# Filling the joints of a four-layer kernel: first steps, last steps, and where square roots and turned tiles go

## The chip, the cores and the metric

The kernel runs on one core of a Trainium2 chip. A core has TensorE (PE; its weight loads are listed apart as PEld), VectorE (DVE), ScalarE (ACT), GpSimd (POOL) and SyncE (SP), which here only issues transfers. Each engine works off its own queue in order. The metric is the time of one execution on the device, in microseconds. The kernel before takes 2728.55 us, the median of three runs (2726.72 to 2733.25).

## The reference, cut to what matters

All is float32. The tokens are x, 16 batches of 100 rows of 512 numbers (1600 rows, 13 tiles of 128 rows). Every batch has its own context of 722 rows of 384 numbers. Four layers are added to x one after the other:

```python
x = x + tanh(g_xattn[0]) * attention0(layernorm(x), ctx)    # 16 heads of 32, biases
x = x + tanh(g_ffn[0])   * experts(layernorm(x))            # 8 experts, the top 2 of each token
x = x + tanh(g_xattn[1]) * attention1(layernorm(x), ctx)    # 8 heads of 64
x = x + tanh(g_ffn[1])   * quantized_ffn(layernorm(x))      # its own residual and normalization inside
```

Attention is queries times keys, softmax, times values, and a projection. The experts' layer picks two experts of each token, computes silu(x w0) * (x w1) wo, and weighs the two results. The last layer is h + 0.5 * (silu(norm(h) w1 + b1) w2 + b2), with w1 and w2 of int32 and a scale for each group of 128 rows, so the input of this layer is normalized twice.

## The kernel before, in words

**Attention (class Attention).** The work is cut into 64 steps: 16 batches of 4 groups m of 128 columns. For a step, `scores` multiplies keys and queries into PSUM (one tile "s"), ACT copies them to SBUF (line 386), and two DVE reductions and a maximum (389, 384) give `mx`. `peaks` turns mx on PE (399) and DVE reduces it to the peak (405). `softmax` spreads the peak on PE (413); DVE subtracts it in two parts (421), ACT takes the exponential of each part (427), and POOL (first attention) or DVE (second) adds up the sums (430). `attend` multiplies with the values (442, 453), and DVE divides (461, 462) into the buffer tT. `project` multiplies a finished tile of 128 tokens with Wo (468) and adds it to x (475).

PE's order is the order in which the program is written. `run` emits, for step i, the peaks of step i, the scores of step i+1, the attend of step i-1, the softmax of step i, and in between a share of other work that does not hang on the chain. That other work is: `extra`, a list of units with a step written beside each (query inputs, queries, projections and whatever the caller adds as `more`), and `todo`, the keys and values of the later batches. Every unit has a `cost` in columns; what is left is divided by the steps that are left, and units of `todo` are added until the share is filled or until their `last` step has come. `cut` puts the first units (2000 columns) ahead of the softmax. Up to `late`, the step before the last but one, an attend follows one step behind; the last three attends are held back. A batch's values come in 6 chunks of 6 matmuls each; its keys in 8 units of 6 matmuls.

**PSUM.** All short products of an attention ("mm") share four tiles in turn: a new one waits until the product four places earlier has been read.

**The other engines' order** is made by a planner, which takes an instruction as soon as its inputs and its buffer are expected to be there, even far ahead of its place in the program. So the last layer's first moments run at 1716 us, long before that layer. A DMA or a POOL instruction that needs SBUF held by an earlier tile waits until that tile's last reader is done: the last layer's pools lie at the same addresses as the second attention's.

**Around the attentions.** `query_input` normalizes a tile of tokens, `transposed` turns it on PE (139) and DVE copies it from PSUM (140). `norm_scales` is a square root on ACT (117), a reciprocal and a product on DVE (118, 119). ACT holds the table of one set of functions: a square root between exponentials is preceded and followed by a table load.

The first attention starts with `first_keys`, values of chunks 0 to 3 of batch 0, `output_bias`, the four query inputs, and the first queries; chunks 4 and 5 follow in step 0. After each group of projected tiles the experts' input is normalized, turned (`Experts.turn`) and multiplied with the gate's weights (`logits`); `top_two` picks the experts, for tiles 0 to 9 in step 60, and for 10 to 12 after the attention, where `places` and `row_map` then sort the tokens. The second attention's run begins with `summed`, which gathers each token's two expert rows by an indirect DMA, adds them to x (970), and takes moments and norm_scales of that one tile; tiles 4 to 12 come in steps 1 to 9.

**The last layer (quantized_ffn)** takes four groups FG of tiles. `normal` takes moments and scales, normalizes a tile on POOL (124), mixes it into x on DVE (1050), takes moments and scales of the result, normalizes on POOL again and adds a bias on POOL (1059). `turn` transposes four 128-column pieces (1071) and DVE writes hT (1076). `weights` loads integers and scales and dequantizes them on DVE (1033); the integers have one buffer. `feed` runs 16 hidden pieces (1095) and their second products (1113).

Of the kernel before, what the change touches and what calls it, by code (L numbers as in the profile page):

```python
# [68 lines left out]
class Layers:  # L69
# [63 lines left out]
    def transposed(self, psum, out, src):  # L133

        nc = self.nc
        n, r = out.shape[1], out.shape[2]
        ps = psum.tile([P, n, r], F32, tag="mm", name="ps_tr")
        for k in range(n):
            nc.tensor.transpose(ps[:, k, :], src[:, k * P : (k + 1) * P], self.ident[:r, :r])  # L139
        nc.vector.tensor_copy(out, ps)  # L140


class Attention:
# [170 lines left out]
    def query_input(self, i, on_act=False, bias=True):  # L314
# [14 lines left out]
        net.transposed(self.ps_m, self.tT[:, :, i * P : i * P + n], xn[:n])  # L329
# [152 lines left out]
    def cost(self, unit):  # L482

        f = unit[0].__name__
        cols = {"values": 6 * C, "keys": 6 * SH, "queries": 8 * GT, "project": 8 * C}
# [10 lines left out]
    def run(self, done=(), after_project=None, more=()):  # L496
# [8 lines left out]
        for g in range(1, B // GB):  # L505
            at = 4 * KC * (g - 1)
            for n, i in enumerate(range(last_tile(g - 1) + 1, last_tile(g) + 1)):
                extra[at + 3 + n].append((self.query_input, i))
# [22 lines left out]
        def last(unit):  # L531

            f, b, n = unit[:3]
            return 4 * b + n - 2 if f == self.keys else 4 * b + (b == B - 1)
# [4 lines left out]
        late = len(steps) - 2  # L539
# [48 lines left out]
class Experts:  # L588
# [71 lines left out]
    def turn(self, psum, p2, i):  # L660
        n = rows_of(i)
        self.xnT[i] = p2.tile([P, KC, P], F32, tag="xnT", name=f"xnT_moe_{i}")
        self.net.transposed(psum, self.xnT[i][:, :, :n], self.xn.pop(i)[:n])
# [318 lines left out]
def quantized_ffn(net, p, gate, out):  # L982
# [3 lines left out]
    with ExitStack() as ctx:  # L986
        pool = lambda n, k, **kw: open_pool(ctx, tc, f"ffn_{n}", k, **kw)

        ps, pq, px, ph, p1, p2 = (
            pool("s", 1), pool("q", 1), pool("x", 4), pool("h", 2), pool("1", 1), pool("2", 2),  # L990
        )
        ps_t, ps_y, ps_z = (pool(n, k, space=PSUM) for n, k in (("t", 2), ("y", 2), ("z", 4)))
        small = {}
        for n in ("gamma_cols", "beta_cols", "b1_cols"):
            small[n] = ps.tile(list(p[n].shape), F32, name=f"ffn_{n}")
            nc.sync.dma_start(small[n], p[n])
        b2 = ps.tile([P, C], F32, name="ffn_b2")
        nc.sync.dma_start(b2, p["b2"].partition_broadcast(P))
        hg = ps.tile([P, 1], F32, name="ffn_hg")
        nc.vector.tensor_scalar(hg, gate, 0.5, None, ALU.mult)  # L1000
        nc.vector.tensor_scalar(b2, b2, hg, None, ALU.mult)
# [35 lines left out]
        xn = {}  # L1037

        def normal(tiles):
# [7 lines left out]
            for i in tiles:  # L1047
                xn[i] = px.tile([P, C], F32, tag="xn", name=f"xn_ffn_{i}")
                net.normalized(nc.gpsimd, xn[i], i)
                nc.vector.scalar_tensor_tensor(  # L1050
                    x[:, i, :], xn[i], gate, x[:, i, :], ALU.mult, ALU.add
                )
            for i in tiles:
                net.moments(i, xn[i])
            net.norm_scales(a, z)
            for i in tiles:
                net.normalized(nc.gpsimd, xn[i], i, xn[i])
# [573 lines left out]
```

## Time and profile before

| what | value |
|---|---|
| median of three runs | 2728.55 us |
| profiled execution, its own time | 2728.79 us |
| its span, first to last instruction | 2727.1 us |
| PE busy | 2682.2 us (98%) |
| mean granted clock of PE | 0.992 |
| first attention | 0 to about 897 us |
| routing | about 897 to 945 us |
| experts | about 945 to 1573 us |
| second attention | about 1573 to 2359 us |
| last layer | about 2359 to 2727 us |

A timeline row reads: start, duration, engine, line, operation, written tile <- read tiles, shape, count, and in brackets the idle time ahead of it with what ended it. In a row of windows the numbers are the stretch, its length, the busy time of PE, PEld, DVE, ACT and POOL with the instructions of each, the granted clock of PE (1.00 is full speed), the share of the DMA engines and GB/s.

### The profile page before, as it was taken

Reading aid. Unit: us, or ns where it says so; the run is one execution under the profiler, and the core shown is the slowest. Engines: PE = TensorE matmul, PEld = TensorE weight load, DVE = VectorE, ACT = ScalarE, POOL = GpSimd, SP = SyncE. Lnnn points to the kernel's source line nnn. Section 1 sums busy time; section 2 is a strip of 40 time slices with the busy share of each in tenths; the row PEclk is TensorE's granted clock in tenths of the full one; section 3 lists DMA queues with packets and bytes.
Section 4 is the critical chain, followed back from the end, with each engine's and each line's share of the span. In section 5 each row is a group of like instructions: output and inputs, shape, how many; then the busy total and the mean of one; then the engine's idle time right before and its main releaser. Section 6 shows DMA issues by size and latency. Waiting matters only on the chain. (4 is left out here: it accounts for less than half of the span.)

```text
span 2727.1 us, 45782 instructions
## 1 busy us (share of the span) xinstructions
PE 2682.2 (98%) x19716; PEld 1739.5 (64%) x19716; DVE 1201.4 (44%) x2010; ACT 860.3 (32%) x1194; POOL 500.2 (18%) x497
## 2 busy tenths in 40 slices
PE   8999999999998999999999999999999999999999
PEld 5666666666565688888888865666666666445554
DVE  4666666666667310101010067656555556711100
ACT  3545554545455100000000045333333334311110
POOL 2544444444442000000000042000000000301000
PEclk9999999999999899999999999999999999999999
DMA  4001000010001499898999522001001010610000
GB/s 167 18 18 34 18 29 22 19 44 18 18 29 58 148 362 353 315 319 314 320 313 317 187 86 68 21 17 34 17 17 34 17 33 1 186 62 16 12 12 10
DMA packets 129189, 278.33 MB, mean 102 GB/s; under 512 B 5824, under 2 KB 5840, under 8 KB 128464
## 3 DMA queue, kind: packets, MB, share of 16 engines
q1 hardware_dynamic: 117888, 246.80, 26.2%
q0 software_dynamic: 5968, 19.17, 2.1%
q10 hardware_dynamic: 5120, 9.31, 0.9%
q8 instruction: 160, 2.62, 0.4%
q14 instruction: 53, 0.43, 0.0%
HBM read 260.31 MB, written 14.94 MB: 101 GB/s over the span
## 5 line engine op out<-in xcount | busy, mean ns | idle before, releaser
L241 PE MATMUL ps_v<-wv_a,ctx_a 128*128 128x512 f32 (+1 forms) x1152 | 520.8, 599 | 1.0 <-DVE pT L421 0.5
L216 PE MATMUL ps_k<-ctx_a,wk_a 128*128 128x361 f32 x1488 | 486.1, 474 | 3.0 <-DVE pT L421 2.3
L887 PE MATMUL ps_h<-xT,w 128*128 128x128 f32 x3712 | 421.8, 276 | 4.0 <-DVEq L1516 4.0
L887 PEld LDWEIGHTS ps_h<-xT,w 128*128 128x128 f32 x3712 | 419.3, 193 | 4.7 <-issue 4.7
L216 PEld LDWEIGHTS ps_k<-ctx_a,wk_a 128*128 128x128 f32 x1488 | 273.6, 190 | 165.7 <-issue 20.5
L241 PEld LDWEIGHTS ps_v<-wv_a,ctx_a 128*128 128x128 f32 (+1 forms) x1152 | 204.2, 184 | 240.9 <-issue 227.4
L427 ACT ACTIVATE pT<-pT 128x1200 f32<-128x1200 f32 (+1 forms) x256 | 243.2, 953 | 248.7 <-DVE pT L421 239.5
L421 DVE TENSOR_TENSOR pT<-raw_a,ps_top 128x400 f32<-128x400 f32 (+4 forms) x384 | 278.7, 770 | 11.5 <-PE ps_top L413 10.4
L430 POOL TENSOR_TENSOR sm<-pT,sm 128x400 f32<-128x400 f32 x244 | 253.0, 1037 | 38.3 <-ACT pT L427 21.6
L389 DVE TENSOR_REDUCE raw_a<-raw_a 128x400 f32<-128x1200 f32 (+1 forms) x128 | 151.9, 1187 | 218.8 <-ACT raw_a L386 218.6
L386 ACT COPY raw_a<-ps_s 128x2000 f32<-128x2000 f32 (+1 forms) x128 | 180.4, 1409 | 154.5 <-PE ps_s L372 154.5
L372 PE MATMUL ps_s<-qT_a,kT_a 32*128 32x100 f32 (+3 forms) x4608 | 213.9, 277 | 1.3 <-DVE qT_a L354 0.7
L898 DVE TENSOR_TENSOR midT<-silu,ps_h 128x512 f32<-128x512 f32 x58 | 39.9, 688 | 389.8 <-PE ps_h L887 376.7
L907 PE MATMUL ps_o<-w,midT 128*128 128x512 f32 x464 | 203.9, 592 | 0.0
L372 PEld LDWEIGHTS ps_s<-qT_a,kT_a 32*128 32x128 f32 (+3 forms) x4608 | 180.1, 180 | 33.4 <-issue 22.9
L1113 PE MATMUL ps_z<-ffn_w,y_ffn 128*128 128x512 f32 (+1 forms) x416 | 190.8, 594 | 0.0
L248 ACT COPY v_a<-ps_v 128x512 f32<-128x512 f32 x192 | 111.5, 582 | 244.5 <-PE ps_v L241 244.5
L1095 PE MATMUL ps_y<-hT,ffn_w 128*128 128x384 f32 (+2 forms) x512 | 183.6, 503 | 0.0
L442 PE MATMUL ps_pv<-pT,v_a 128*32 128x100 f32 (+3 forms) x4608 | 160.7, 252 | 5.2 <-ACT pT L427 5.0
L1095 PEld LDWEIGHTS ps_y<-hT,ffn_w 128*128 128x128 f32 x512 | 95.1, 190 | 84.6 <-issue 50.3
L907 PEld LDWEIGHTS ps_o<-w,midT 128*128 128x128 f32 x464 | 85.9, 190 | 97.1 <-issue 97.1
L389 DVE TENSOR_REDUCE mx<-raw_a 128x400 f32<-128x1200 f32 (+1 forms) x128 | 146.7, 1146 | 0.5
(169 smaller groups left out, 2199.9 us busy)
## 6 DMA issues: line engine op xcount, KB each, us to landing
w<-in_L_ffn_w SPq DMA_DIRECT2D x116, 1024.0 KB, 6.4
w<-in_L_ffn_wo SPq DMA_DIRECT2D x29, 2048.0 KB, 10.5
ctx_a<-in_ctxT SPq DMA_DIRECT2D x30, 1083.0 KB, 5.3
q<-in_L_ffn_fc_q SPq DMA_DIRECT2D x8, 1024.0 KB, 5.2
ffn_w<-in_L_ffn_fc_scales SPq DMA_DIRECT2D x8, 1024.0 KB, 12.2
rows<-ot ACTq DMA_DIRECT2D x29, 256.0 KB, 6.9
xn_d<-xn_moe POOLq DMA_DIRECT2D x11, 256.0 KB, 2.6
ctx_a<-in_ctxT SPq DMA_DIRECT2D x6, 361.0 KB
```

Of the source, the lines that this page charges most:

```text
L216: nc.tensor.matmul(ps, self.wk[:, k, m * P : (m + 1) * P], self.cxs[b][:, k, c * SH : (c + 1) * SH], start=(k == 0), stop=(k == KK - 1),)
L241: nc.tensor.matmul(ps[:n], self.cxs[b][:, k, c * P : c * P + n], self.wv[:, k, :], start=(k == 0), stop=(k == KK - 1),)
L372: nc.tensor.matmul(ps[:r, j, n * T : (n + 1) * T], self.kT[b, m][j * D : (j + 1) * D, c * P : c * P + r], self.qT[g][j * D : (j + 1) * D, ...
L386: nc.scalar.copy(st[:, :, :NS1, :].rearrange("p g c t -> p g (c t)"), ps[:, :, : NS1 * T])
L389: nc.vector.tensor_reduce(to, st[:, :, c : c + 3, :].rearrange("p g c t -> p g t c"), AX.X, ALU.max)
L421: nc.vector.tensor_tensor(t[:, part, :, c:z, :], st[:, :, at : at + z - c, :], bcast(ps.unsqueeze(2), P, G, z - c, T), ALU.subtract,)
L427: nc.scalar.activation(t[:, part], t[:, part], AF.Exp)
L430: adds.tensor_tensor(sm, t[:, part, :, n, :], sm if part or n > 1 else t[:, 0, :, 0, :], ALU.add)
L887: nc.tensor.matmul(ph[:, f, :], w[:, n, k, f * P : (f + 1) * P], self.xT[j][:, k, :], start=(k == 0), stop=(k == KC - 1),)
L907: nc.tensor.matmul(po, self.midT[j, f // 4][:, f % 4, :], w[:, f, :], start=(f == 0), stop=(f == KF - 1),)
L1095: nc.tensor.matmul(ps[:, :nt], w1[f // nf][:, k, f % nf * P : (f % nf + 1) * P], hT[g][:, k, :nt], start=(k == 0), stop=(k == KC - 1),)
L1113: nc.tensor.matmul(z[j][:n], y[:, j * P : j * P + n], w2[f // nf][:, f % nf, :], start=(f == 0), stop=(f == NF - 1),)
```

## The change

1. `transposed` may copy on ACT instead of DVE. The query inputs of the first attention (G is 4 there) and all turned tiles of the experts' routing do so.
2. The cost of a unit of queries over a part of the columns is that of these columns.
3. The query inputs of later groups come one step later (4 instead of 3 steps behind the group's start).
4. In the first attention the last batch's values are due one step earlier, and no attend is held back (`late` lies behind the last step).
5. Batch 0's values in the first attention: chunk 3 between the turned tokens 1 and 2, chunk 4 before the first queries, chunk 5 between these and the first scores; none in step 0.
6. `top_two` splits at tile 7 instead of 10 (EARLY), so its first part comes in step 44.
7. In the second attention the scales of tiles 4 to 12 are taken in two groups, tiles 4 to 6 in step 4 and 7 to 12 in step 11.
8. A class FirstTokens does what the last layer did for its first group of tiles inside the second attention, in steps 30 to 63: small loads, moments, mixing, second moments, normalization and bias, and the turning in steps 60 to 63. Its tiles have a pool of their own on the right side of SBUF; the buffer of the second attention's query weights, on the same side, is now kept to the end. The last layer starts with its weights and the first products.

```diff
-    def transposed(self, psum, out, src):
+    def transposed(self, psum, out, src, on_act=False):
...
-        nc.vector.tensor_copy(out, ps)
+        (nc.scalar.copy if on_act else nc.vector.tensor_copy)(out, ps)
...
-        net.transposed(self.ps_m, self.tT[:, :, i * P : i * P + n], xn[:n])
+        net.transposed(self.ps_m, self.tT[:, :, i * P : i * P + n], xn[:n], self.G == 4)
...
+        if f == "queries" and len(unit) > 3:
+            return 8 * (unit[4] - unit[3])
...
-                extra[at + 3 + n].append((self.query_input, i))
+                extra[at + 4 + n].append((self.query_input, i))
...
-            return 4 * b + n - 2 if f == self.keys else 4 * b + (b == B - 1)
+            return 4 * b + n - 2 if f == self.keys else 4 * b + (b == B - 1 and self.G == 2)
...
-        late = len(steps) - 2
+        late = len(steps) - 2 if self.G == 2 else len(steps) + 1
...
-        self.net.transposed(psum, self.xnT[i][:, :, :n], self.xn.pop(i)[:n])
+        self.net.transposed(psum, self.xnT[i][:, :, :n], self.xn.pop(i)[:n], True)
...
+class FirstTokens:
...
+    def mix(self, i, pool=None):
+
+        net, nc = self.net, self.net.nc
+        xn = self.xn[i] = (pool or self.pool).tile([P, C], F32, tag="xn", name=f"xn_ffn_{i}", bufs=4)
+        net.normalized(nc.gpsimd, xn, i)
+        return nc.vector.scalar_tensor_tensor(
+            net.x[:, i, :], xn, self.gate, net.x[:, i, :], ALU.mult, ALU.add
+        )
...
+    def units(self, psum):
+
+        tiles = FG[0]
+        units = [(30, self.load), (34, self.scale)]
+        for n, i in enumerate(tiles):
+            units += [
+                (36 + n, self.net.moments, i),
+                (41 + n, self.mix, i),
+                (44 + n, self.again, i),
+                (50 + n, self.normal, i),
+                (52 + n, self.bias, i),
+            ]
+        units += [(s, self.net.norm_scales, tiles[0], tiles[-1] + 1) for s in (40, 48)]
+        units += [
+            (KC * B - KC + k, self.turn, psum, "mm", self.pool, 0, tiles, k) for k in range(KC)
+        ]
+        return units
...
-        normal(FG[0])
         with tc.manual_schedule(engines={PE}):
-            for k in range(KC):
-                turn(0, FG[0], k)
...
-EARLY, LATE = 10, 11
+EARLY, LATE = 7, 11
...
-                for c in range(4):
+                for c in range(3):
                     a0.values(0, c)
-                    if c == 2:
-                        a0.output_bias()
+                a0.output_bias()
                 for i in range(4):
                     a0.query_input(i, bias=False)
+                    if i == 1:
+                        a0.values(0, 3)
...
+                a0.values(0, 4)
                 a0.queries(0, 0)
+                a0.values(0, 5)
                 more = [(-1, a0.queries, 0, m) for m in range(1, KC)]
-                more += [(0, a0.values, 0, c) for c in range(4, NS)]
...
-                pr = open_pool(c1, tc, "a1_q", side="right")
+                pr = open_pool(ctx, tc, "a1_q", side="right")
...
-                net.norm_scales(i, i + 1)
+                if i < 4:
+                    net.norm_scales(i, i + 1)
...
+            more += [(4, net.norm_scales, 4, 7), (11, net.norm_scales, 7, NTT)]
+            pf = open_pool(ctx, tc, "ffn_f", side="right")
+            first = FirstTokens(net, p, tgf[:, 1:2], pf)
+            more += first.units(a1.ps_m)
```

## The prediction

> **What bounds the kernel now.** I read the page's busy shares first, then the table of 20 us windows over the whole span, then the timeline wherever TensorE (PE) stood idle. The windows show which joints cost time:
>
> ```profile
> PE 2682.2 (98%) x19716; PEld 1739.5 (64%) x19716; DVE 1201.4 (44%) x2010; ACT 860.3 (32%) x1194; POOL 500.2 (18%) x497
> ...
> 20.00:40.00 20.00, 18.34 (x57) 9.00 (x56) 10.53 (x27) 5.67 (x12) 5.19 (x7) 1.00 0.49 169
> 420.00:440.00 20.00, 18.06 (x158) 11.11 (x156) 10.97 (x15) 6.00 (x7) 10.40 (x10) 0.91 0.00 1
> 820.00:840.00 20.00, 17.54 (x214) 10.84 (x202) 19.12 (x33) 9.54 (x11) 8.89 (x9) 1.00 0.00 1
> 860.00:880.00 20.00, 13.70 (x276) 9.81 (x280) 10.88 (x15) 7.22 (x7) 0.00 (x0) 0.83 0.54 191
> 1580.00:1600.00 20.00, 17.73 (x106) 11.34 (x106) 13.42 (x33) 8.16 (x14) 11.75 (x12) 0.95 0.64 197
> 1640.00:1660.00 20.00, 18.52 (x140) 12.06 (x140) 12.37 (x30) 12.88 (x20) 7.52 (x7) 0.91 0.26 91
> 2320.00:2340.00 20.00, 16.41 (x136) 9.99 (x136) 14.73 (x24) 5.45 (x9) 9.92 (x8) 0.97 0.65 159
> ```
>
> After the stretch come PE, PEld, DVE, ACT and POOL busy, the granted clock and the DMA. PE is busy 2682.2 of 2727.1 us, so 44.9 us of idleness is all there is to win, plus the half-speed stretches that follow some stalls. By windows the idleness is: 4.7 us in the first load, 2.4 at 20-60, 4.5 at 380-440 and 560-600, 3.6 at 760-860, 9.6 at 860-920 (end of the first attention), 4.0 at 940-960 (a branch), 6.3 at 1560-1700 (start of the second attention), 5.4 at 2320-2380 (into the last layer), 4.4 in the final store. The change touches all but the first load, 380-440, 560-600, the branch and the store: 27 us. The timeline names the waits (idle before, and its releaser, in brackets):
>
> ```profile
> 36.10 1.41 PE L139 MATMUL ps_tr<-ident,xn_a 128*128 128x128 f32 x8 [0.56 <-POOL xn_a L124]
> 38.50 2.95 PE L345 MATMUL ps_q<-tT_a,wq_a 128*128 128x400 f32 x8 [1.00 <-DVE tT_a L140]
> 42.18 1.37 PE L372 MATMUL ps_s<-qT_a,kT_a 32*128 32x100 f32 x40 [0.73 <-DVE qT_a L354]
> ...
> 430.86 5.33 PE L468 MATMUL ps_y<-wo_a,tT_a 128*128 128x512 f32 x8 [1.94 <-DVE pT L421]
> 838.16 0.61 PE L399 MATMUL ps_mx<-ident,mx 128*100 128x128 f32 x4 [1.27 <-DVE mx L384]
> 870.49 1.09 PE L399 MATMUL ps_mx<-ident,mx 128*100 128x128 f32 x4 [5.97 <-DVE mx L384]
> ...
> 1597.55 0.43 PE L399 MATMUL ps_mx<-ident,mx 128*100 128x128 f32 x2 [1.70 <-DVE mx L384]
> 1640.22 1.28 ACT L117 ACT_TABLE_LOAD   x1
> 1641.83 1.28 ACT L427 ACT_TABLE_LOAD   x1
> 1643.88 0.74 PE L442 MATMUL ps_pv<-pT,v_a 128*64 128x100 f32 x12 [0.51 <-ACT pT L427]
> 2337.56 0.40 PE L399 MATMUL ps_mx<-ident,mx 128*100 128x128 f32 x2 [3.42 <-DVE mx L384]
> ```
>
> **What a stall costs.** The 8 matmuls behind the 1.94 us stall at 430.86 take 5.33 us; eight of that shape take 3.46 elsewhere. The clock over 426-436 is 0.83, so 3.4 us ran at half speed, a loss of 1.7 us. The stalls of 1.70, 0.51+0.96 and 3.42 us show the same loss; those of 1.27 (838) and 0.89+0.46 us (1695) do not. I price a stall of about 1.5 us or more at itself plus 1.7. The Trainium skill, "TensorE: Matmul & The Clock Gate", section "What's actually happening", has the clock fall only after an idle window of some 3.4 us. By that rule the three removable stalls below would cost no clock, and the sum would be 5.1 us smaller in gain; the trace has the loss after 1.5 to 1.9 us, so the rows decide.
>
> **The change, part by part.**
>
> First steps of the first attention. Chunks 3, 4 and 5 of batch 0's values (2.6 us of PE each, 6 matmuls of 0.43) now stand between turned tokens 1 and 2, before the queries, and between queries and scores: in front of the waits of 0.56, 1.00 and 0.73 us. Each is longer than its wait: gain 2.3, bounds 0 and 2.4. Chunks 4 and 5 used to fill step 0; the share rule puts keys of batch 1 there instead, whose context lands well before 50 us.
>
> Copies of turned tiles move to ACT in the first attention and the routing: 0.59 us (row of v_a, same shape) instead of 0.62 to 0.69 on DVE. ACT is busy 9 to 12 of 20 us there and no PE wait names either. I take 0; it could win the 0.78 us wait on DVE L140 at 888.95 or lose some 0.5 at 901, where ACT first issues two DMAs (1.26 us).
>
> Top-two split at 7 instead of 10. In routing it works on 6 tiles, not 3: three more adds of 0.19, and 11 operations 0.03 longer, 0.9 us on DVE; PE's ps_n starts 0.1 us after that chain now, so 0.9 is lost. The early part (now 6.3 us of DVE in steps 59-60, with PE stalls of 1.18 and 1.27) goes to step 44 and shrinks to 4. Steps there last 12.8 us against 11.9, so I take 0.7 of new stall, between 0 and 2.5 plus 1.7 of clock.
>
> End of the first attention. Attends are no longer held back, and the last batch's values come a step sooner. Before step 61 PE gets one value unit more (2.8 us) and loses the 2.45 of stalls: 0.35 later. From there the max-and-softmax chain sets the pace (850.07 to 860.16 to 870.49, 10 us a step, both with PE idle), so early attends only fill the 5.97 us hole. At the very end DVE's subtract waited 0.88 us for a score tile held by a late attend; that goes. Net 0.5 gained. The 1.6 us of top-two makes this and the last paragraph together 1.1 lost, bounds 5 lost and 4 gained.
>
> Start of the second attention. Queries of 100 and 300 columns were counted as 400; counted right, two key units (4 us) move into step -1, in front of the 1.70 stall. The stall and its 1.7 of clock go, but step 0 loses those units and its chain (mx ready 1607.1 now, stretched by DVE's combines) may show: 2.7 net. Nine square roots become two. The one at 1641.51, with its two table loads, sits between two halves of an exponential and costs 0.51+0.96+1.7 = 3.2; the one at 1692.68 costs 1.35. Both go; the group of tiles 4 to 6 remains at about the same place, though behind the exponentials in program order: half of 3.2 charged. And query inputs moved a step later keep the POOL normalization ahead of PE. Together 2.7+3.2+1.35-1.6 = 5.65, bounds 0 and 9.9 (all idleness and clock there).
>
> First tokens of the last layer inside the second attention. Moments, mixing, two root visits and POOL work for tiles 0 to 3 move to steps 36 to 55, windows with PE idle 0.0 and DVE 11 to 13 of 20 us busy: hidden behind keys and values; each root visit delays exponentials by 2.9 us (1.28+0.29+1.28), against 3.7 us between the exponentials' end (2307.45) and their attend (2311.16). Cost 0; without that cover 3.2 each. The 16 turns (2.2 us of PE) move into steps 60 to 63 and their DVE copies (4 x 0.78) with them. What leaves the end: the four mixes that held DVE L389 until 2333.55 though its input was ready at 2329.76 (stall 3.42, clock 1.7), the root's table loads (stall 1.21), 0.17, and the 0.53 between turns: 7.0. Late next are the weights: the second tile's integers load behind the first dequantization and are ready about 11.3 us after it; with no turns ahead, z wants them some 2.8 us sooner, against 2.3 us of slack now: 0.5. Another 0.5 for the copies in DVE's chain. Gain 6.0, bounds 2 and 7.5.
>
> **Sum.** 2.3 - 1.1 + 5.65 + 6.0 = 12.9 us. The profiled execution took 2728.79 us (span 2727.1 and 1.7 around it), 0.2 above the median of 2728.55, so no correction: 2715.9, say 2716.
>
> **Rivals.**
> *B, the second attention's start keeps its stalls* (DVE's combines wait for gathered rows in order, and the change leaves them): 2716+5.65 = 2721.5.
> *C, the root visits stall.* Steps 4, 11, 40 and 48 each cost the 3.2 us seen at 1641: 1.6 + 3x3.2 = 11.2 more, 2727. Against it: seven of the nine visits now show no stall that large. The Trainium skill, "ScalarE: Activation LUTs", section "What ACT_TABLE_LOAD costs", adds a drain of 1.38 us to each 1.28 us load; a visit would then delay 5.6 us, outlast the 3.7 us and make C certain. The trace has the root start at 1610.59, 0.02 us after its load ended, so I leave C low.
> *D, the slower side: the last layer's first weights come late.* Its small tiles (2.1 KB) leave the bottom of memory and every tile there slides down. The first scales' load now issues at 2320.41, into the old values. Slid down, it overlaps the last context, free at 2327.2: landing 12.2 later, 2339.4, still early. If it had to wait for the last project (2352.8 in the new timing), dequantization (2.28) would end at 2367.3: 14.5 of stall, 3.4 of clock (as behind the 5.97 stall), 2.8 more for the second tile: 2736.7. It decides from an issue after 2338; each us later costs one.
> *E, better:* moving query inputs a step and copies to ACT also frees the 1.94 us stalls at 428.9 and 595.4. For it only that these steps turn tiles; against it, their releaser is the subtract L421. 7.3 us more: 2708.7.
>
> **How the numbers follow.** Likeliest case 0.55, 2716, its own range 2710 to 2721; B 0.18; C 0.10; D 0.12; E 0.05. 0.3%, or 8.2 us, is about what can be told from no change: 2720.4 and 2736.7 are the limits. Faster: nine tenths of the likeliest (0.49), a third of B (0.06), all of E: 0.60. Slower: D's upper half (0.06) and 0.04, taken from the likeliest, for stalls at the moved places that no row names. Same: the remaining 0.30. The range of 2707 to 2728 leaves out D, half of C and the lower part of E, about 0.19.
>
> **What would show it.** Right: no PE wait over 0.3 us at 34-45; none on mx near 1597 or on pT near 1643; two root visits for tiles 4 to 12; mx of the last step not late; no turns between the last project and the first ps_y. Wrong: a wait of ps_y or ps_z on a dequantization, a new wait of 1.5 us or more near step 44, step 0 of the second attention or steps 60 to 63, or a half-speed stretch where none was.

## The result, and where the time went

The changed kernel takes 2715.7 us (median; 2714.38 to 2718.82) where the kernel before, timed beside it, takes 2728.23. The ratio is 0.9951, with a 95% interval of 0.994 to 0.9962: 12.5 us less. The profiled execution took 2714.80 us with a span of 2712.9, so 14.2 us of span went. The sum of the prediction was 12.9. This agreement hides terms that are wrong in both directions: as a sum it is luck.

The page's line of busy shares and the table of windows of the changed kernel (after the stretch: PE, PEld, DVE, ACT and POOL busy, granted clock, DMA share, GB/s):

```profile
PE 2675.3 (99%) x19716; PEld 1735.7 (64%) x19716; DVE 1190.8 (44%) x1970; ACT 853.1 (31%) x1199; POOL 496.2 (18%) x497
...
20.00:40.00 20.00, 20.00 (x62) 10.03 (x61) 7.91 (x23) 8.77 (x18) 4.99 (x7) 1.00 0.55 184
420.00:440.00 20.00, 19.27 (x189) 12.96 (x185) 11.94 (x16) 8.69 (x10) 10.02 (x10) 1.00 0.18 57
820.00:840.00 20.00, 20.00 (x214) 11.18 (x213) 16.20 (x17) 11.03 (x14) 8.61 (x9) 1.00 0.00 1
860.00:880.00 20.00, 14.68 (x280) 10.47 (x273) 11.37 (x23) 5.78 (x6) 1.35 (x2) 0.93 0.15 58
1580.00:1600.00 20.00, 15.70 (x119) 11.51 (x120) 17.58 (x36) 9.38 (x17) 14.38 (x14) 1.00 0.52 171
2320.00:2340.00 20.00, 18.79 (x230) 13.35 (x228) 12.89 (x27) 7.25 (x10) 0.00 (x0) 1.00 0.73 211
```

PE is idle for 37.6 us where it was idle for 44.9. The window at 420 us, which no step of the sum touched, went from 18.06 to 19.27 us busy and from a clock of 0.91 to 1.00. The window at 1580 us, in the stretch for which the sum had 5.65 of gain, went from 17.73 to 15.70. (The work in a window is no longer quite the same, since it comes earlier.) The rows of PE that answer to those shown of before:

```profile
36.19 1.04 PE L139 MATMUL ps_tr<-ident,xn_a 128*128 128x128 f32 x8
39.65 2.85 PE L345 MATMUL ps_q<-tT_a,wq_a 128*128 128x400 f32 x8
...
427.54 3.70 PE L468 MATMUL ps_y<-wo_a,tT_a 128*128 128x512 f32 x8 [0.73 <-ACT xnT_moe L140]
...
852.18 0.92 PE L399 MATMUL ps_mx<-ident,mx 128*100 128x128 f32 x4 [2.13 <-DVE mx L384]
863.64 0.65 PE L399 MATMUL ps_mx<-ident,mx 128*100 128x128 f32 x4 [1.34 <-DVE mx L384]
...
1576.40 0.66 PE L139 MATMUL ps_tr<-ident,xn_a 128*128 128x128 f32 x4 [1.70 <-ACT xn_a L318]
1599.19 0.40 PE L399 MATMUL ps_mx<-ident,mx 128*100 128x128 f32 x2 [3.29 <-DVE mx L384]
1635.54 0.39 PE L453 MATMUL ps_pv<-sm,ones 128*64 128x100 f32 x4 [1.56 <-DVE sm L430]
1708.95 0.45 PE L453 MATMUL ps_pv<-sm,ones 128*64 128x100 f32 x4 [2.00 <-DVE sm L430]
1910.96 0.39 PE L453 MATMUL ps_pv<-sm,ones 128*64 128x100 f32 x4 [1.04 <-DVE sm L430]
...
2327.64 0.39 PE L399 MATMUL ps_mx<-ident,mx 128*100 128x128 f32 x2
2337.86 1.33 PE L442 MATMUL ps_pv<-pT,v_a 128*64 128x100 f32 x24 [1.21 <-ACT pT L427]
2347.36 7.13 PE L1140 MATMUL ps_y<-hT,ffn_w 128*128 128x512 f32 x16
```

The first rows have lost their waits, and so has mx of the last step (2327.64, where before stood 3.42 us). The projection at 427.54 waits 0.73 us for ACT instead of 1.94 for DVE, and its eight matmuls take 3.70 us instead of 5.33. In the second attention there are five waits that were not there or were smaller.

A running difference tells where the 14.2 us lie: the start of the same piece of PE's work in the changed kernel's trace less its start in the trace of before. Each number is the difference of two starts.

| PE's work | before | after | difference |
|---|---|---|---|
| first attention, peaks of step 28 | 407.45 | 405.33 | -2.1 |
| step 30 | 439.67 | 434.72 | -5.0 |
| step 43 | 616.95 | 610.31 | -6.6 |
| steps 45 to 58 | | | -8.1 |
| first keys of the second attention | 897.05 | 885.48 | -11.6 |
| first product of the experts | 944.67 | 932.45 | -12.2 |
| first values after the experts | 1573.64 | 1561.59 | -12.1 |
| second attention, first turned token | 1586.97 | 1576.40 | -10.6 |
| step 11 | | | -9.4 |
| step 29 | | | -7.6 |
| last attend | 2349.27 | 2337.86 | -11.4 |
| first product of the last layer | 2361.60 | 2347.36 | -14.2 |

So the first attention and the routing gained 12.2, of which 6.5 between steps 27 and 58, almost all at two places that the sum had put at nothing; the second attention lost 4.5 up to step 29, where 5.65 had been expected as gain; its end and the entry into the last layer gained 6.7.

### The profile page after: what moved, and what is told of

It reads as the page before. It is cut to its first block, busy times and chain, and to the rows that moved or that the text cites. A ratio compares the mean times of both kernels' runs of the same rounds, so it can differ in the third digit from the quotient of the medians.

```text
span 2712.9 us, 45740 instructions
## 1 busy us (share of the span) xinstructions
PE 2675.3 (99%) x19716; PEld 1735.7 (64%) x19716; DVE 1190.8 (44%) x1970; ACT 853.1 (31%) x1199; POOL 496.2 (18%) x497
## 5 line engine op out<-in xcount | busy, mean ns | idle before, releaser
L421 DVE TENSOR_TENSOR pT<-raw_a,ps_top 128x400 f32<-128x400 f32 (+4 forms) x384 | 279.1, 770 | 14.5 <-PE ps_top L413 14.3
L372 PE MATMUL ps_s<-qT_a,kT_a 32*128 32x100 f32 (+3 forms) x4608 | 215.1, 279 | 1.5 <-ACT raw_a L386 1.1
L372 PEld LDWEIGHTS ps_s<-qT_a,kT_a 32*128 32x128 f32 (+3 forms) x4608 | 181.0, 182 | 34.1 <-issue 23.2
```

Source lines behind the costliest of these rows:

```text
L372: nc.tensor.matmul(ps[:r, j, n * T : (n + 1) * T], self.kT[b, m][j * D : (j + 1) * D, c * P : c * P + r], self.qT[g][j * D : (j + 1) * D, ...
L421: nc.vector.tensor_tensor(t[:, part, :, c:z, :], st[:, :, at : at + z - c, :], bcast(ps.unsqueeze(2), P, G, z - c, T), ALU.subtract,)
```

## The experiments

For each experiment the running difference is taken against the changed kernel's trace (or before's, where said), which shows at which step its time differs. Up to the first difference between two programs it stays within about 0.2 us over hundreds of microseconds, except where it is said otherwise: in the first keys of e2, at one wait for a load, and at the joint told of at the end.

The times alone tell less. The changed kernel's ratio to before has the interval 0.994 to 0.9962. Only e1's interval lies apart from it, and e2's lies apart from 1, the kernel before; all the others overlap that of the changed kernel. So the gains and losses of e3 to e12 rest on one pair of profiles each.

### The two stalls of 1.94 us: copies on ACT, or query inputs a step later

One of the two stood ahead of a projection, the other ahead of a unit of keys (597.38 in the kernel before). The theory after seeing the result was that ACT's copies had removed them (A). The rival was the later step of the query inputs (B). Three kernels set them apart.

e1_copies_dve, every copy on DVE again:

```diff
-        (nc.scalar.copy if on_act else nc.vector.tensor_copy)(out, ps)
+        nc.vector.tensor_copy(out, ps)
```

> The changed kernel with every turned tile copied by DVE again, all else as changed. Theory A (the two stalls of 1.94 us before a projection, at 428.9 and 595.4, were turned tiles whose copy stood on DVE behind the subtract; ACT's copies freed them): both stalls come back with their half-speed stretches, about 3 us each, near steps 29 and 42 of the first attention, so about 2722 us, 6.4 more than the changed kernel. Theory B (the query inputs' later step freed them): no stall over 1 us at those steps and 2716, within 1.5 us.

e2_before_act, the kernel before with these copies alone:

```diff
-    def transposed(self, psum, out, src):
+    def transposed(self, psum, out, src, on_act=False):
...
-        nc.vector.tensor_copy(out, ps)
+        (nc.scalar.copy if on_act else nc.vector.tensor_copy)(out, ps)
...
-        net.transposed(self.ps_m, self.tT[:, :, i * P : i * P + n], xn[:n])
+        net.transposed(self.ps_m, self.tT[:, :, i * P : i * P + n], xn[:n], self.G == 4)
...
-        self.net.transposed(psum, self.xnT[i][:, :, :n], self.xn.pop(i)[:n])
+        self.net.transposed(psum, self.xnT[i][:, :, :n], self.xn.pop(i)[:n], True)
```

> The kernel before with the copies of turned tiles on ACT in the first attention and the routing, nothing else. Theory A (these copies alone free the two stalls): about 2722 us, 6.4 less than before, gained at steps 29 and 42 of the first attention and nowhere else by more than 1 us. Theory B (the later step of the query inputs is needed): 2728, within 1.5 us.

e3_query_step, the query inputs at their old step:

```diff
-                extra[at + 4 + n].append((self.query_input, i))
+                extra[at + 3 + n].append((self.query_input, i))
```

> The changed kernel with the query inputs of later groups back at 3 steps behind the group's start. Theory A (ACT's copies freed the two stalls): 2716 us within 1.5, and no stall over 1 us at steps 29 and 42. Theory B (the later step freed them): about 2722, 3 us lost near each of these steps.

Measured: e1 2721.39 us (ratio to before 0.9977, 0.9967 to 0.9987), e2 2721.41 (0.9975, 0.9965 to 0.9985), e3 2714.93 (0.9953, 0.9936 to 0.9969). Against the changed kernel e1 loses 3.3 us between steps 27 and 30 and 2.4 between 39 and 42, and stands at 5.9 afterwards. Both stalls are back in it:

```profile
429.35 4.05 PE L468 MATMUL ps_y<-wo_a,tT_a 128*128 128x512 f32 x5 [1.93 <-DVE pT L421]
...
598.30 3.88 PE L216 MATMUL ps_k<-ctx_a,wk_a 128*128 128x361 f32 x12 [1.93 <-DVE pT L421]
```

Against before, e2 gains 3.35 us between steps 27 and 30 and as much between 39 and 42, and nothing else over 0.1 us from step 0 to 63 (it begins 1.0 late: its first keys take 17.59 us, not 16.23). e3 differs by 0.1 us at the end, and no wait over 0.73 us stands between its steps 20 and 46. Theory A holds. How a copy on another engine frees a projection is seen in the timeline, first of the kernel before:

```profile
427.94 2.77 DVE L421 TENSOR_TENSOR pT<-raw_a,ps_top 128x1200 f32<-128x1200 f32 x3
428.29 0.63 PE L139 MATMUL ps_tr<-ident,xn_moe 128*128 128x128 f32 x4
...
432.50 0.68 DVE L140 COPY xnT_moe<-ps_tr 128x512 f32<-128x512 f32 x1
```

and of e2:

```profile
428.46 2.78 DVE L421 TENSOR_TENSOR pT<-raw_a,ps_top 128x1200 f32<-128x1200 f32 x3
...
429.54 0.59 ACT L140 COPY xnT_moe<-ps_tr 128x512 f32<-128x512 f32 x1 [2.30 <-PE ps_tr L139]
...
430.17 3.70 PE L468 MATMUL ps_y<-wo_a,tT_a 128*128 128x512 f32 x8 [0.73 <-ACT xnT_moe L140]
```

The projection needs one of the four PSUM places "mm". In the kernel before all four were held by products that DVE reads: the spread peak (`ps_top`, read by the subtract L421 until 430.71), an attend, logits, and the turned token, whose copy stood in DVE's queue until 432.50. The first to come free was that of the peak, so L421 was indeed the releaser. With the copy on ACT the turned token's place is free at 430.13 while L421 still runs to 431.24, and the projection takes that place instead: it starts at 430.17, while the product four places earlier, the spread peak, is still being read. So the places are not simply taken in turn, as the description of the kernel has it. The first read of the releaser was right; it was not the only one that could have released the wait.

### The cost of a query unit

e4_query_cost:

```diff
-        if f == "queries" and len(unit) > 3:
-            return 8 * (unit[4] - unit[3])
```

> The changed kernel with every unit of queries counted as 400 columns again, so that the second attention's first steps get their keys where they had them before. Theory A (the truer cost only moves the stall from step -1 to step 0, where mx comes late as well): 2716 us, within 1.5; a stall of about 1.7 us ahead of step 0's peaks and less than 1.5 us ahead of step 1's, instead of 3.3 there. Theory B (the sum of the prediction): the cost is worth 2.7 us, so about 2718.5.

Measured: 2715.54 us (ratio 0.9958, 0.9941 to 0.9975). In the profiles e4 is ahead by 1.3 us from step 2 of the second attention on. PE's rows of e4 where the changed kernel has 3.29 us:

```profile
1586.86 0.43 PE L399 MATMUL ps_mx<-ident,mx 128*100 128x128 f32 x2 [1.71 <-DVE mx L384]
...
1594.93 3.91 PE L216 MATMUL ps_k<-ctx_a,wk_a 128*128 128x361 f32 x12 [1.75 <-DVE tT_a L140]
1599.27 0.40 PE L399 MATMUL ps_mx<-ident,mx 128*100 128x128 f32 x2 [0.43 <-DVE pT L421]
```

The idle time is the same, 1.71 + 1.75 + 0.43 = 3.9 us here and 0.65 + 3.29 in the changed kernel. The two key units only move it from ahead of step 0 to ahead of step 1, where DVE's chain is as late, and put it together into one stall with a half-speed stretch behind it (24 matmuls of L372 in 2.46 us, elsewhere 1.53). Theory A holds; the truer cost is worth nothing, or about -1.3.

### The groups of square roots, and who slows the sums

e5_single_roots:

```diff
-                if i < 4:
-                    net.norm_scales(i, i + 1)
+                net.norm_scales(i, i + 1)
...
-            more += [(4, net.norm_scales, 4, 7), (11, net.norm_scales, 7, NTT)]
```

> The changed kernel with a square root for each of tiles 4 to 12 again, right behind the tile's moments, instead of the two groups. Theory A (the groups traded stalls: the one for tiles 4 to 6 and the missing root near 1692 saved about 3.2 us, the one for tiles 7 to 12 lost 3.7 at step 11): 2716 us, within 1.5; the stall of 2.0 us at step 11 is gone and stalls on exponentials near steps 5 and 9 are back. Theory B (the prediction's sum): grouping is worth 2.95 us, so about 2718.7.

e8_no_bias:

```diff
-            if bias:
+            if bias and self.G == 4:
                 self.add_bias(i)
```

> The changed kernel without the output bias of the second attention on tiles 4 to 12 (one addition of 128x512 on POOL for each of these tiles is left out, so the tokens lack that bias; a measurement of what the additions cost). Theory A (DVE's three sums of exponentials at 1632 and 1705, 3.2 us instead of 1.2, are slow because POOL adds at the same time): they take 1.2 to 1.6 us, the stall of 2.0 us and its half-speed stretch at step 11 and the 1.56 us stall at step 5 go or fall under 0.5, and the kernel takes about 2710.5 us. Theory B (the sums are slow or late because of the square root ahead of them): they stay above 2.5 us or the stalls stay, 2715.7 within 1.

Measured: e5 2713.19 us (ratio 0.9953, 0.9936 to 0.9969), e8 2711.05 (0.9933, 0.9916 to 0.995). By the running difference single roots gain 0.6 at step 5, lose 1.8 at step 9 and gain 3.7 at step 11: e5 stands 3.3 us ahead from there, 0.8 of them from steps 0 and 1, where a load landed 0.6 us earlier (told of below). In the pair of profiles, then, grouping cost 2.5 us, against a gain of 2.95 in the sum; theory A's even trade was too kind to it. The reason is in the sums of exponentials, three DVE additions of 128x200. The tile `sm` on DVE from 1600 to 1720 us in the changed kernel (ns, least/median/most):

```profile
L430 DVE TENSOR_TENSOR sm<-pT,sm x44: 354/366/1524, 1600.4 to 1716.5; 128x200 f32<-128x200 f32 x44
```

the same in e8, without the bias additions,

```profile
L430 DVE TENSOR_TENSOR sm<-pT,sm x44: 355/366/543, 1604.6 to 1715.3; 128x200 f32<-128x200 f32 x44
```

and in e5:

```profile
L430 DVE TENSOR_TENSOR sm<-pT,sm x44: 351/366/369, 1599.8 to 1713.2; 128x200 f32<-128x200 f32 x44
```

What runs beside the slow ones in the changed kernel:

```profile
1705.69 3.21 DVE L430 TENSOR_TENSOR sm<-pT,sm 128x200 f32<-128x200 f32 x3 [0.92 <-ACT pT L427]
...
1705.96 2.72 POOL L334 TENSOR_TENSOR x<-x,gbo_a 128x512 f32<-128x512 f32 x2
```

A group makes several tiles ready at once. POOL then normalizes and adds the bias to two tiles back to back, just when the exponentials are done that the root held up, and DVE's additions wait. In e8, which leaves out the bias additions for tiles 4 to 12 and has the same order of instructions on PE, DVE and ACT, the three sums take 1.17 and 1.34 us at the two places, with the root ahead of them as before:

```profile
1708.02 1.34 DVE L430 TENSOR_TENSOR sm<-pT,sm 128x200 f32<-128x200 f32 x3 [0.92 <-ACT pT L427]
```

e8 gains 1.8 us at step 5 and 3.5 at step 11, 5.3 together; theory A's 5.2 for these places is met. So at these two places the visits to the root table do not stall PE by themselves; POOL's additions do, by holding up DVE's. The Trainium skill, "SBUF — State Buffer", section "SBUF: two separate sides", says that an instruction of VectorE with two inputs in SBUF and one of GpSimd that reads SBUF exclude each other for a whole instruction, whichever starts first; the changed kernel's trace agrees, with a sum of 1.52 us at most, 1.16 over its median, beside POOL additions of 1.36 each (2.72 for two).

Elsewhere a visit does stall PE: the 1.8 us that e5 loses at step 9 begin with PE waiting for an exponential behind a single root, and no sum there is slow:

```profile
1682.37 0.74 PE L442 MATMUL ps_pv<-pT,v_a 128*64 128x100 f32 x12 [0.89 <-ACT pT L427]
```

### What the planner took early

e6_pin_load keeps the last layer's small loads and the scaling of its bias in program order:

```diff
-            nc.sync.dma_start(self.small[n], p[n])
+            self.net.tc.keep_in_program_order(nc.sync.dma_start(self.small[n], p[n]))
...
-        nc.sync.dma_start(self.b2, p["b2"].partition_broadcast(P))
+        self.net.tc.keep_in_program_order(
+            nc.sync.dma_start(self.b2, p["b2"].partition_broadcast(P))
+        )
...
+        keep = self.net.tc.keep_in_program_order
+        keep(nc.vector.tensor_scalar(self.hg, self.gate, 0.5, None, ALU.mult))
+        keep(nc.vector.tensor_scalar(self.b2, self.b2, self.hg, None, ALU.mult))
```

> The changed kernel with the small loads of the last layer and the scaling of its bias kept at their places in the program (steps 30 and 34) instead of being taken early by the planner, at 1564 to 1572 us. Theory A (there they delay the first gathered rows and stand ahead of their moments on DVE): the wait of 1.70 us ahead of the first turned token falls to about 0.2, and the kernel takes about 2714.2 us, 1.5 less than the changed one. Theory B (the gathered rows are late for another reason, or the next wait takes the gain): 2715.7 within 0.7.

e7_pin_first keeps the first tokens' two roots there (`norm_scales` returns its activation for this):

```diff
-        units += [(s, self.net.norm_scales, tiles[0], tiles[-1] + 1) for s in (40, 48)]
+        units += [
+            (s, self.kept, self.net.norm_scales, tiles[0], tiles[-1] + 1) for s in (40, 48)
+        ]
...
+    def kept(self, f, *a):
+        self.net.tc.keep_in_program_order(f(*a))
```

> The changed kernel with the two square roots of the last layer's first tokens kept at their places in the exponentials' order (steps 40 and 48), instead of steps 27 and 28 where the planner took them. Theory A (1.9 us were lost because both visits, the mixes and the second moments fell into the same two steps on DVE and POOL): the loss at steps 26 to 29 goes, at steps 40 to 50 less than 0.7 is lost, about 2714 us. Theory B (each visit costs its stall wherever it stands): the loss moves to steps 40 to 50, 2715.7 within 0.7.

Measured: e6 2713.36 us (ratio 0.9949, 0.9932 to 0.9965), e7 2712.01 (0.9945, 0.9929 to 0.9962). e7 loses nothing at steps 40 to 50 and gains 1.9 at steps 28 and 29: theory A. e6's first turned token follows its first values by 13.4 us, not 14.8, with this wait in place of 1.70:

```profile
1577.90 0.66 PE L139 MATMUL ps_tr<-ident,xn_a 128*128 128x128 f32 x4 [0.33 <-ACT xn_a L318]
```

and about 1.2 of these 1.4 us are kept by step 2. e6 gains 1.9 at steps 28 and 29 as well, which was not expected: its two roots are still early there (their table loads start at 1896.55 and 1910.80), but without the scaled bias POOL can't add it to the tokens at that time. So at this place, too, the loss goes when POOL's additions leave, with the roots where they were.

In e7 the start of the second attention is 1.4 us faster, although its programs of DVE and ACT are the same there. DVE's queue waits for the load of the attention's own output bias, and that load landed later in the profiled execution of the changed kernel:

```profile
1589.61 0.49 DVE L312 TENSOR_SCALAR gbo_a<-gbo_a,tgx 128x512 f32<-128x512 f32 x1 [1.68 <-DMA gbo_a<-in_L_xattn_bo]
```

than in e7:

```profile
1588.19 0.49 DVE L313 TENSOR_SCALAR gbo_a<-gbo_a,tgx 128x512 f32<-128x512 f32 x1
```

This wait lasts 1.68 us in the profile of the changed kernel, 1.19 in e4, 1.05 in e5, 0.31 in e6 and 0.11 in e7. The figures of 1.3 and 1.2 us for e4 and e6 are no larger than this scatter; their mechanisms are seen in the waits, their sizes are not certain.

### The first steps, the split of the top two, and the ends

e10_starts undoes the first steps and the split:

```diff
-EARLY, LATE = 7, 11
+EARLY, LATE = 10, 11
...
-                for c in range(3):
+                for c in range(4):
...
-                    if i == 1:
-                        a0.values(0, 3)
...
-                a0.values(0, 4)
                 a0.queries(0, 0)
-                a0.values(0, 5)
...
+                more += [(0, a0.values, 0, c) for c in range(4, NS)]
```

> The changed kernel with batch 0's values where they were in the first attention's first steps, and the top-two split at tile 10 again. Theory A (the running difference): 1.6 us lost by step 9, nothing at step 44, 2.4 lost at steps 59 and 60 where the larger top-two stands again, 0.9 won in routing: about 2718.8 us. Theory B (the prediction's terms): 2.3 lost by step 9, 0.7 won at step 44, the 2.4 at step 60 swallowed by the chain of the last steps, 0.9 won in routing: about 2716.4.

e11_ends undoes the end of the first attention, and moves the turns of the last layer's first tokens behind the last projection:

```diff
-            return 4 * b + n - 2 if f == self.keys else 4 * b + (b == B - 1 and self.G == 2)
+            return 4 * b + n - 2 if f == self.keys else 4 * b + (b == B - 1)
...
-        late = len(steps) - 2 if self.G == 2 else len(steps) + 1
+        late = len(steps) - 2
...
-            (KC * B - KC + k, self.turn, psum, "mm", self.pool, 0, tiles, k) for k in range(KC)
+            (KC * B + KC + k, self.turn, psum, "mm", self.pool, 0, tiles, k) for k in range(KC)
```

> The changed kernel with the end of the first attention as before (the last attends held back, the last batch's values due a step later) and the turns of the last layer's first tokens behind the second attention's last projection. Theory A (the end of the first attention is worth about 3 us by the running difference, and the turns stand openly on PE, 2.7 us): about 2721 us. Theory B (the prediction's terms, 0.5 for the end of the first attention and 2.7 for the turns): about 2719.

Measured: e10 2720.35 us (ratio 0.9962, 0.9948 to 0.9976), e11 2722.43 (0.9971, 0.9958 to 0.9983). e10 loses 1.9 us by step 9, wins 0.4 at step 44, loses 2.45 at steps 59 and 60, where the stalls of before return,

```profile
818.99 0.62 PE L399 MATMUL ps_mx<-ident,mx 128*100 128x128 f32 x4 [1.18 <-ACT pT L427]
831.59 0.62 PE L399 MATMUL ps_mx<-ident,mx 128*100 128x128 f32 x4 [1.27 <-DVE mx L384]
```

and wins 0.86 in routing (`ps_n`). Up to step 60 that is theory A. But at the peaks of step 63 only 0.4 of the 2.45 is left, as theory B has it, and what follows lies in the joint, where one program differs from itself by more than this. The time, 3 us more than the changed kernel by the ratios, is A's, and its interval holds B's 0.7 as well. So which of the two holds stays open. In the e11 profile steps 61 to 63 come 2.6 to 3.8 us sooner and the old stall is back,

```profile
859.88 1.09 PE L399 MATMUL ps_mx<-ident,mx 128*100 128x128 f32 x4 [5.97 <-DVE mx L384]
```

but the second attention's first keys come 0.3 later and its step 0 is 0.2 sooner: early or late attends make no difference that this pair shows. Theory A's 3 us are not seen in it, though at this joint a difference of that size could be hidden. The entry into the last layer alone accounts for the whole of e11's loss:

```profile
2346.17 3.09 DVE L1039 TENSOR_SCALAR hT<-ps_hT,ffn_gamma_cols,ffn_beta_cols 128x512 f32<-128x512 f32 x4 [6.71 <-PE ps_hT L1034]
2349.18 2.28 DVE L1110 SCALAR_TENSOR_TENSOR ffn_w<-q,ffn_w 128x2048 f32<-128x2048 int32 x1
```

```profile
2351.52 10.08 PE L1140 MATMUL ps_y<-hT,ffn_w 128*128 128x512 f32 x16 [3.10 <-DVE ffn_w L1110]
```

The four copies stand ahead of the dequantization on DVE, PE waits 3.10 us for the weights, and 3.0 more are lost at half speed (10.08 us for 16 matmuls that take 7.13 in the changed kernel). Both theories priced the turns at 2.7 us of PE's time; the order on DVE that they bring costs more than twice that, so neither described what happened. This is how the weights can come late: not from memory, but behind other work in the queue.

### Putting the savings together

e9_joined has the edits of e4, e5, e6 and e7 in one kernel.

> The changed kernel with four edits together: every unit of queries counted as 400 columns again, one square root for each of tiles 4 to 12 again, the last layer's small loads and bias scaling kept at steps 30 and 34, and the first tokens' two roots kept at steps 40 and 48. Theory A (the four savings measured one by one, 1.3, 3.3, 1.3 and 1.9 us by the running difference, lie at different places and add up): 2708 us, within 1.5. Theory B (three of them act on the same chain of the second attention's first steps and overlap): about 2711.

e12_more adds two to it:

```diff
-                for i in range(1, 4):
-                    summed(i)
+                summed(1)
...
+            more = [(-1, summed, 2), (0, summed, 3)] + more
...
-            net.norm_scales(a, z)
+            ins = net.norm_scales(a, z)
+            tc.keep_in_program_order(ins)
```

> The four edits joined, and two more: the second attention's tiles 2 and 3 are gathered and summed one and two steps later, and the square roots of the last layer's later groups are kept in program order, behind the last exponentials. Theory A (the 1.70 us stall of step 0 is DVE standing in these sums, and the 1.21 us ahead of the last attend is the root taken early): both go, 2.9 us less than the four edits alone, about 2705 to 2709 us and a ratio to before of 0.992 to 0.993. Theory B (the chain of step 0 waits for something else and later sums make the next query inputs late): the end gains 1.2, the start loses up to 2, ratio about 0.9935 as for the four edits.

Measured: e9 2712.4 us (ratio 0.9935, 0.9919 to 0.9952; 2707.49 to 2713.97), e12 2709.49 (0.9932, 0.9918 to 0.9946; 2709.03 to 2715.03). e9's profiled execution is the one of 2707.49 us; in it the running difference to the changed kernel is -2.8 at step 3, -5.25 at step 11 and -7.1 from step 29 to the end, near the 7.8 of theory A. The median is nearer to theory B's 2711. By the ratios e9 is 0.0016 below the changed kernel, some 4 us, and the intervals overlap: a gain that the profiles place, but that the times alone do not prove. In e12 the 1.21 us ahead of the last attend are gone and 1.2 us are won there, but the later sums bring a new wait at the start, larger than the one of 1.70 they removed:

```profile
1606.93 0.60 PE L454 MATMUL ps_pv<-sm,ones 128*64 128x100 f32 x4 [4.42 <-DVE sm L431]
```

From first values to step 2 e12 needs some 2.5 us more than e9. By the profiles, e12's being the slowest of its five executions, that is theory B; the times fit either.

## Why the prediction was right, point by point

The forecast of 2716 us with 2707 to 2728 met 2715.7. The terms did not meet theirs, and that the sum came out is luck: 6.5 us that it had put at nothing, and some 5 beyond its terms at the joint before the experts, made up for the 10 by which the second attention fell short of its two terms.

| step of the prediction | predicted gain | found |
|---|---|---|
| first steps | 2.3 | 1.6 (pair of traces), 1.9 (e10) |
| copies to ACT | 0 | 6.5 (pair), 5.8 (e1), 6.7 (e2), up to step 58 |
| top two and end of the first attention | -1.1 | between -0.9 and +1.2 (0.4 to 2.45 - 0.4 - 0.86, e10); attends not to be told from 0 (e11) |
| start of the second attention | 5.65 | -2.6 |
| first tokens in the middle | 0 | -1.9 |
| end, entry into the last layer | 6.0 | 6.7 |

*First steps.* Right. The three waits are gone; a new one of 0.45 us on mx stands at 65.73 us, in a step that gave up a unit of values.

*Copies to ACT.* The step that failed is the sentence of rival E, "against it, their releaser is the subtract L421". The mechanism of E is what happened, at a chance of 0.05. The releaser was read rightly; the fault was to conclude that nothing else could release the wait, when it was a wait for any of four places and the change moved the reader of another one.

*Top two, end of the first attention.* The routing cost was right (0.9 predicted, 0.86 found), that at step 44 was half of the 0.7. The step that set the two stalls at steps 59 and 60 against an added value unit held: the stalls went (2.5 us by step 60) and step 61 gave back 2.6, so it comes 0.1 late where 0.35 was predicted. What is left of this at the end, and the net 0.5 for the attends, lies within what a pair of profiles can't tell. The pair has 4.1 us at this joint, more than these terms. Some 1.7 of them may be clock: PE ran 23.9 us at half speed there before and 20.5 after. The section on the hardware says why no such number can be read from one pair.

*Start of the second attention.* Four steps failed, all in one direction, worse than rival B. "The stall and its 1.7 of clock go": they moved one step on (e4). "Both go; the group of tiles 4 to 6 remains at about the same place": the groups cost 2.5 us against single roots (e5). The sum had put the price of a visit on the root and its table alone. That was right for the 1.35 us, which return in e5 (0.89 and 0.46 us of waits at step 9); what it left out are POOL's additions, which several ready tiles let loose together (e8). They could be read in the kernel before: its three sums at 1643.86 took 1.67 us beside an addition of POOL, where three of the median length take 1.1. "Its small loads" were counted for memory and not for place: the planner took them to 1564 us, ahead of the first gathered rows (e6). The bound of 0 at the lower end of this term had no reason behind it; a loss was possible and should have been inside. The prediction's own signs of being wrong say the same: a wait on mx near 1597 and a new wait of 1.5 us or more about step 0 of the second attention both stand in the profile (1599.19, 1576.40).

*First tokens in the middle.* "Hidden behind keys and values" was argued for the steps written in the list, 36 to 55. The planner ran them at steps 27 and 28, both visits, the mixes and POOL's additions together, and 1.9 us showed. At their own steps they are hidden, as the prediction had it (e7).

*End.* Right in mechanism, and in size to within 0.7: mx of the last step has no wait, no turn stands between the last projection and the first product. The wait of 1.21 us for a root's table stays, since the next group's root was taken early instead (2330.63); e12 removes it and wins 1.2. Without this 1.21 and without the two charges of 0.5 each the working gives 5.8, so 0.9 of the 6.7 found belongs to no term.

*Rivals.* B came true in that the start kept its stalls, and was exceeded; of its cause no run shows more than a part, since in the changed kernel DVE's queue waits 1.68 us for the load of the attention's bias as well. C (root visits stall): one at 2.00 us with a half-speed stretch at step 11, one of 1.56 at step 5, none at steps 40 and 48 in e7; the Trainium skill's drain of 1.38 us ("ScalarE: Activation LUTs", section "What ACT_TABLE_LOAD costs") is not seen here either: the root at 1629.87 starts 0.02 us after its load ends. D (weights late): did not happen; the scales' load was issued at 2320.92, against 2320.41 before, and e11 shows the other way to it.

*The price of a stall,* "about 1.5 us or more at itself plus 1.7", was too regular. Half-speed stretches follow 2.00 and 3.29 us, none follows 1.70 (1576.40), 1.56 (1635.54), 1.71 and 1.75 in e4, or 2.12 in e10 (856.17). What decides is how the stall lies in time; the last section has it.

## What to carry to other kernels

A releaser names what ended a wait, not what it needed: if the wait is for one of several buffers, look at who reads each of them, and count moving any one reader off a busy queue as a possible gain. When a planner orders the engines, price a moved unit where it will be ready, not at the step written beside it, and pin what must stay. Before grouping small work to save table loads, ask what the group sets free all at once on the other engines.

## What the runs showed of the hardware

The additions of DVE with two inputs in SBUF go from 0.37 to 1.52 us beside additions on POOL, while the work of PE beside them is untouched; the prediction had POOL as free cover.

The same program does not run through the joint between the first attention and the experts in the same time. The changed kernel, e6 and e8 have the same program up to 1560 us and start their experts' first product at 932.45, 935.36 and 938.94. Windows over the joint of the changed kernel, e6 and e8:

```profile
850.00:945.00 95.00, 81.53 (x651) 55.74 (x651) 39.32 (x102) 22.56 (x33) 6.79 (x8) 0.89 0.45 158
```

```profile
850.00:945.00 95.00, 82.04 (x624) 55.47 (x625) 37.75 (x99) 22.29 (x32) 5.83 (x7) 0.86 0.42 146
```

```profile
850.00:945.00 95.00, 81.84 (x602) 52.98 (x602) 38.57 (x100) 21.81 (x32) 5.84 (x7) 0.84 0.37 131
```

PE is busy for the same time, but at clocks of 0.89, 0.86 and 0.84 (20.5, 27.3 and 30.7 us at half speed), and gets less done in it (651, 624 and 602 matmuls).

The clock records of the profiles show when half speed is granted. In each of the fourteen traces all half-speed stretches between the first steps and the final store start whole multiples of 3.413 us apart and last whole multiples of it: in the changed kernel at 852.41 (10.2 us long), 917.26 (3.4), 930.91 (6.8), 1599.93 and 1709.15 (3.4 each). The Trainium skill, "TensorE: Matmul & The Clock Gate", section "What's actually happening", has the clock decided in windows of 3.4 us that run freely and do not start with the kernel; the traces agree with that in the lengths and in the starts. Laying this grid over PE's rows shows that idle time counts by window: between 60 and 2700 us, and outside 870 to 925, every window at full speed with 1.81 us or more of idleness was followed by half speed, none with 1.46 or less was, and between these both happened. From 870 to 925 us half speed also followed windows with less, so this is not the whole rule. It does tell stalls of like size apart. The 1.70 us that end at 1597.55 in the kernel before lie within one window and cost speed; the 1.70 that end at 1576.40 in the changed kernel are cut by an edge at 1576.04 and cost none.

So the same stall can cost 1.7 us more or nothing, by where it falls on a grid that the program doesn't set. That this is why one program takes different times over the joint fits the records, but no run tests it. The consequence stands in the runs: a difference of up to 6.5 us at this joint can come from the execution, the times of one kernel spread over 2 to 8 us, and differences that a running comparison places at a step are safe to about 0.2 us only away from this joint and from waits for a transfer.
